# Storing u four times and loading it as 32 rows, partitions ordered images by states

## The chip, the cores and the metric

The kernel runs on one core of a Trainium2 chip. The metric is the device time of one execution in microseconds (us). The program is one launch; all 16 DMA engines of the core and its five instruction queues (PE for matmuls, DVE, ACT, POOL and SP) belong to it alone.

## What is computed

The reference is a network of four layers on an input of 64 images, each of 11 x 11 positions and 128 channels. Every layer has two parts with a residual around each: a mixer, which is the same in all four layers, and a feed-forward part, which differs (a mixture of experts, twice a recurrent net, and a spectral convolution). The change touches the mixer alone. Cut to what matters, it is:

```python
xz = x @ in_proj_w.T                                   # x: 64 images, 121 positions, 128 channels
xc, z = jnp.split(xz, 2, axis=-1)                      # 256 each
xc = conv_general_dilated(xc as (B, 121, 256), conv_w, (1,), [(1, 1)])   # in the kernel: 121 "channels", 256 steps
t = silu(xc + conv_b)
xs = stack([t, t], axis=1)                             # K = 2 directions
x_dbl = einsum('bkdl,kcd->bkcl', xs, x_proj_w)
dts, Bs, Cs = x_dbl[:, :, :8], x_dbl[:, :, 8:24], x_dbl[:, :, 24:]
delta = softplus(einsum('bkrl,kdr->bkdl', dts, dt_proj_w) + dt_proj_b)
A = -exp(A_logs).reshape(2, 121, 16)                   # 16 states
dA = exp(delta[..., None] * A)
dBu = delta[..., None] * Bs * xs[..., None]
h[l] = dA[l] * h[l - 1] + dBu[l]                       # along the 256 steps
y = einsum('bkdln,bknl->bkdl', h, Cs) + Ds * xs
out = layernorm(y[:, 0] + flip(y[:, 1])) * gelu(z) @ out_proj_w.T
```

With `u = delta * t`, the scan's input is `u * B`, where `u` depends on image, channel and step, and `B` on image, state and step. So each row of `u` is needed for all 16 states.

## The kernel before

The mixer is the class `Conv`. It takes the 64 images in 8 groups of `CB` = 8, and each group in two directions, so there are 16 pairs (group `c`, direction `k`), numbered `m`. A scan fills the 128 partitions with 8 images times 16 states. In the order before, partition `p` is state `p // 8` and image `p % 8` (states by images).

For one `m` there are 121 channels, taken in pairs: 61 steps of two channels, 512 elements a partition. A step of the main loop in `run` is:

- `rows` (L677, PE): two matmuls that spread `delta` from the three bf16 parts in `R` onto the 128 partitions of `da`; `pick` holds the matrices that choose the rows.
- `exps` (L690, ACT): two exponentials in place on `da`, with the scale `A`.
- `scan` (L698, DVE): one scan over 512 elements, `da` and `ub` into `H`.
- `by_c` (L719, PE): matmuls of `H` with `Cz`, which sum over states; `keep_y` (L734 DVE, L736 ACT) takes their results out.

`u` reaches the scan by way of DRAM. `steps` computes, for two images at a time, `delta` and `u` with channels on partitions (`u`, L339, on POOL), and its `store` (L353 and L354) writes `delta` to `dD` and `u` to `uD`. `uD` is laid out as `[group, direction, image, 128 channels, 256]`. Then `load_u` (L654) brings 4 channels of all 8 images into one `ub` tile of 128 x 1024 elements: 8 rows of 4096 bytes, repeated for 16 states. There are `UB` = 7 such buffers. `times_b` (L666, POOL) multiplies `ub` in place by `Bt`. For one `m` that makes 31 tiles (30 of 4 channels and one of a single channel).

Other loads of the mixer: `load_bc` (L636) loads `Bt` and `Cp`, both as (state, image) rows from `bcD`; `load_r` (L627, L629) loads `R` from `dD`; `tail` loads `ts` from `sD` (L453) and `y` from `yD` (L455) for the group before, transposes and normalizes them (L460, L468, L474) and projects; `last` (L552 `sD`, L559 `yD`) does that for the last group of a layer. `begin` (L206) loads the next group's `x`.

The order is written out by hand. `at` and `lay` put closures on a plan by step numbers, and `run` plays it: for step `g` the matmuls and exponentials of `g + 3` come first, then `load_u` and `times_b` due at this step, then the scan, then what the plan holds. `load_u` of a tile is put 14 steps ahead of its first scan, `times_b` 5 steps. Each engine executes its own instructions in the order of the program, and all of these DMAs are issued from SP, so a DMA that waits holds those behind it. `steps` of a group's first direction start at step 49 of the group before, 11.6 steps apart for each two images; those of the second direction at 95. In the first group of a layer, `steps(0, 0, ...)` runs ahead of the loop, alone. The tiles `d` and `u` of `steps` have two buffers each.

```python
        self.nc.sync.dma_start(
            x[:, :n, :].rearrange("p d l -> p (d l)"),
            self.uD[m // 2, m % 2, :, 4 * i : 4 * i + n, :]
            .rearrange("b d l -> b (d l)")
            .unsqueeze(0)
            .to_broadcast([NS, CB, n * L]),
        )
```

These are the lines of `load_u` before. The functions that the diff touches follow whole.

Of the kernel before, what the change touches and what calls it, by code (L numbers as in the profile page):

```python
# [8 lines left out]
F32 = mybir.dt.float32  # L9
BF16 = mybir.dt.bfloat16  # L10
AF = mybir.ActivationFunctionType
ALU = mybir.AluOpType
AX = mybir.AxisListType
# [3 lines left out]
D = 121  # L17
C = 128
L = 256
NS = 16  # L20
# [18 lines left out]
def bcast(ap, n):  # L39

    return ap.unsqueeze(2).to_broadcast([ap.shape[0], ap.shape[1], n])
# [36 lines left out]
CB = 8  # L78
# [2 lines left out]
TILES = 31  # L81
STEPS = 2 * PAIRS
RING = 5
UB = 7


class Conv:
# [9 lines left out]
    def weights(self, setup, fixed, ps):  # L97
        cx, nc, a = self.cx, self.nc, self.cx.a
        p = f"L{self.l}_conv_"

        def load(pool, name, shape, src):
            t = pool.tile(shape, F32, name=name)
            nc.sync.dma_start(t, src)
            return t

        in_x = load(setup, "in_x", [128, 2, C], a[p + "in_x"].rearrange("(q p) c -> p q c", p=128))
        conv_wT = load(
            setup, "conv_wT", [128, 3, 2, L], a[p + "conv_wT"].rearrange("j (q p) o -> p j q o", p=128)
        )
        x_dt = load(setup, "x_dt", [8, 2, D], a[p + "x_dt"])  # L110
        dt_wT = load(setup, "dt_wT", [8, 2, D], a[p + "dt_wT"])
        self.Ds = fixed.tile([128, 2], F32, name="Ds")
        nc.vector.memset(self.Ds, 0.0)
        nc.sync.dma_start(self.Ds[:D], a[p + "Ds"])
        self.in_zT = load(fixed, "in_zT", [C, L], a[p + "in_zT"])
        self.conv_b = load(fixed, "conv_b", [1, L], a[p + "conv_b"])
        self.x_bc = load(fixed, "x_bc", [D, 4 * NS], a[p + "x_bc"])
        self.norm = load(fixed, "norm", [D, 2], a[p + "norm"])
        self.out_wT = load(fixed, "out_wT", [128, 2, C], a[p + "out_wT"].rearrange("(q p) c -> p q c", p=128))

        self.A = fixed.tile([128, 2, D], F32, name="A")
        for k in range(2):
            nc.sync.dma_start(self.A[:, k, :], a[p + "A_logs"][k].unsqueeze(1).to_broadcast([NS, CB, D]))
        return lambda: self.made(setup, fixed, ps, in_x, conv_wT, x_dt, dt_wT)

    def made(self, setup, fixed, ps, in_x, conv_wT, x_dt, dt_wT):
        cx, nc, a = self.cx, self.nc, self.cx.a
        p = f"L{self.l}_conv_"
        af = self.A.rearrange("p k d -> p (k d)")
        nc.scalar.activation(af, af, AF.Exp)  # L130
        nc.vector.tensor_scalar_mul(af, af, -1.0)


        pick = setup.tile([5 * 24, 5, CB], F32, name="pick")
        nc.vector.reduce_sum(pick, cx.ident[:120, :120].rearrange("p (a s b) -> p a b s", s=3, b=CB), axis=AX.X)
        self.pick = fixed.tile([5 * 24, 5, NS, CB], BF16, name="pick16")
        for i in range(5):
            nc.vector.tensor_copy(self.pick[:, i], pick[:, i, :].unsqueeze(1).to_broadcast([120, NS, CB]))

        self.w_conv = fixed.tile([C, 3, L], F32, name="w_conv")  # L140
        for j in range(3):
            pw = ps.tile([C, L], F32, name="pw", tag="mm")
            for q in range(2):
                nc.tensor.matmul(pw, in_x[:, q, :], conv_wT[:, j, q, :], start=(q == 0), stop=(q == 1))
            nc.scalar.copy(self.w_conv[:, j, :], pw)


        self.w_dt = fixed.tile([D + 1, 2, 128], F32, name="w_dt")
        nc.vector.memset(self.w_dt, 0.0)
        nc.sync.dma_start(self.w_dt[D : D + 1, :, :D], a[p + "dt_b"].unsqueeze(0))  # L150
        for k in range(2):
            pw = ps.tile([D, D], F32, name="pdt", tag="mm")
            nc.tensor.matmul(pw, x_dt[:, k, :], dt_wT[:, k, :], start=True, stop=True)
            nc.scalar.copy(self.w_dt[:D, k, :D], pw)
        self.one = fixed.tile([128, 1], F32, name="one")
        nc.vector.memset(self.one, 1.0)
        self.ones = fixed.tile([1, 128], F32, name="ones")
        nc.vector.memset(self.ones, 1.0)

        self.own = fixed.tile([128, CB], F32, name="own")  # L160
        nc.vector.reduce_sum(self.own, cx.ident.rearrange("p (n b) -> p b n", b=CB), axis=AX.X)

    def buffers(self, fixed, work, ps_f, dram):
        cx, nc, NC = self.cx, self.nc, self.NC
        self.work = work

        self.H = [fixed.tile([128, 2 * L, 16], F32, name="H"), cx.HX.rearrange("p (a w) -> p a w", w=16)]
        self.spare = [x.rearrange("p a w -> p (a w)") for x in self.H]
        self.da = [ps_f.tile([128, 2, L], F32, name=f"da{i}") for i in range(RING)]
        self.yb = ps_f.tile([128, 8, 2, 2, 16], F32, name="yb")  # L170
        nc.vector.memset(self.yb, 0.0)
        self.Cz = [fixed.tile([128, 64, CB], F32, name=f"Cz{i}") for i in range(4)]
        self.t = fixed.tile([128, CB, L], F32, name="t")
        nc.gpsimd.memset(self.t, 1.0)  # L174
        self.xnT = [fixed.tile([C, CB, D + 2], F32, name=f"xnT{i}") for i in range(2)]
        for x in self.xnT:
            nc.gpsimd.memset(x[:, :, 0 : D + 2 : D + 1], 0.0)
        self.yst = fixed.tile([128, 64, D], F32, name="yst")
        self.uD = dram.tile([NC, 2, CB, 128, L], F32, name="uD")
        self.dD = dram.tile([NC, 2, 128, 3, CB, L], BF16, name="dD")  # L180
        self.bcD = dram.tile([NC, 4 * NS, CB, L], F32, name="bcD")
        self.sD = dram.tile([NC, 128, CB, L], F32, name="sD")
        self.yD = dram.tile([NC, L, CB * D], F32, name="yD")
# [99 lines left out]
    def steps(self, c, k, start, apart, late):  # L283


        nc, work, out = self.nc, self.work, []
        alone = c == 0 and k == 0
        for b in range(0, CB, 2):
            s = {}
# [61 lines left out]

            def store(b=b, s=s):
                nc.sync.dma_start(self.dD[c, k, :, :, b : b + 2, :].rearrange("d s b l -> d s (b l)"), s["d"])  # L353
                nc.sync.dma_start(  # L354
                    self.uD[c, k, b : b + 2].rearrange("b d l -> d b l"), s["u"].rearrange("p (b l) -> p b l", l=L)
                )

            at = start + b // 2 * apart
            for i, f in enumerate((project, parts, e, ln, less, delta, first)):
# [2 lines left out]
            for i, f in ((late, u), (late + 1, rest), (late + 2.5, second), (2 * late + 2, third), (2 * late + 4, store)):  # L362
                out.append((at + i, f))
# [267 lines left out]
    def load_bc(self, m):  # L631
        c, k = m // 2, m % 2
        for name, at in (("Bt", 0), ("Cp", NS)):
            x = self.work.tile([128, L], F32, name=name, bufs=2)
            r0 = 2 * NS * k + at
            self.nc.sync.dma_start(x, self.bcD[c, r0 : r0 + NS].rearrange("r b l -> (r b) l"))  # L636
            self.bc[m, name] = x

    def own_c(self, m, u):
# [9 lines left out]
    def load_u(self, T):  # L649
        m, i = divmod(T, TILES)  # L650
        n = min(4, D - 4 * i)
        x = self.work.tile([128, 4, L], F32, name="ub", bufs=UB)
        self.ub[T] = x
        self.nc.sync.dma_start(  # L654
            x[:, :n, :].rearrange("p d l -> p (d l)"),
            self.uD[m // 2, m % 2, :, 4 * i : 4 * i + n, :]
            .rearrange("b d l -> b (d l)")
            .unsqueeze(0)
            .to_broadcast([NS, CB, n * L]),
        )  # L660

    def times_b(self, T):
# [8 lines left out]
    def rows(self, g):  # L671

        m, p = divmod(g, PAIRS)
        for j in range(self.channels(p)):
            d = 2 * p + j
            n = 24 if d == D - 1 else 120
            self.nc.tensor.matmul(  # L677
                self.da[g % RING][:, j, 1:],
                self.pick[:n, d % 5].rearrange("p n b -> p (n b)"),
                self.R[m, d // 35][:n, d % 35 // 5, 1:],  # L680
                start=True,
                stop=True,
            )

    def exps(self, g):
        m, p = divmod(g, PAIRS)
        for j in range(self.channels(p)):
            x = self.da[g % RING][:, j, 1:]
            d = 2 * p + j
            self.nc.scalar.activation(x, x, AF.Exp, scale=self.A[:, m % 2, d : d + 1])  # L690

    def scan(self, g):
# [6 lines left out]
            self.H[dq % 2][:, :n, p - DQ[dq][0]],  # L699
            self.da[g % RING].rearrange("p j l -> p (j l)")[:, :n],  # L700
            x.rearrange("p d l -> p (d l)")[:, 2 * j * L : 2 * j * L + n],
# [668 lines left out]
def metaformer_kernel(ctx: ExitStack, tc: tile.TileContext, a: dict, out: bass.AP):  # L1370
# [28 lines left out]
    cx.KD = dram.tile([R0[3], C * C], F32, name="KD")  # L1399
    v, kept, passing, weights = mixer(0)  # L1400
    weights()()
    passing.close()
    for l in range(4):
# [70 lines left out]
```

## Time and profile before

| | |
|---|---|
| Median of 3 runs | 8451.34 us (8445.54 to 8459.70) |
| Span of the profiled execution | 8458.2 us, between its first and last instruction |
| Busy PE, DVE, ACT, POOL | 5994.4, 6141.0, 5768.7, 5832.5 us |
| DMA moved | 1603.70 MB, mean 190 GB/s |
| `ub<-uD` loads | 1920 of 512 KB and 64 of 128 KB |
| `uD<-u` stores | 256 of 256 KB |
| `dD<-d` stores, `R<-dD` loads | 256 of 384 KB; 192 of 420 KB and 64 of 180 KB |
| Multiply by B, L666 | 1984, 2317 ns in the mean |
| Scan, L698 | 3904, some 1200 ns each |

The profile shows one execution; its span is 6.9 us over the median of the runs and inside their spread. No other time of that execution is given. Where the profile cuts the span in 40 slices, each is 211 us long. The four mixers with their scans are the stretches from about 80 to 1720, 2090 to 3720, 4038 to 5680 and 5995 to 7620 us; the feed-forward parts and the start of the next mixer lie between and behind.

### The profile page before, as it was taken

How to read it: one execution, taken by the hardware profiler on the slowest of the kernel's cores; microseconds unless marked ns; L12 is line 12 of the kernel's file. 1: busy time of each engine (PE TensorE's matmuls, PEld its weight loads, DVE VectorE, ACT ScalarE, POOL GpSimd, SP SyncE). 2: the span in 40 equal slices, each digit the busy share in tenths (PEclk: the TensorE clock that was granted, in tenths of full speed). 3: DMA queues.
4: the chain of work that ended last, by engine and by line, in shares of the span. 5: the costliest groups of instructions: out<-in, count | busy, mean ns of one | idle time of the engine just before them, and what ended most of it. 6: DMA issues, size and time to landing. Idle time of an engine off the chain costs nothing.

```text
span 8458.2 us, 209204 instructions
## 1 busy us (share of the span) xinstructions
PE 5994.4 (71%) x83374; PEld 3445.8 (41%) x83374; DVE 6141.0 (73%) x8636; ACT 5768.7 (68%) x12927; POOL 5832.5 (69%) x3139
## 2 busy tenths in 40 slices
PE   5676677676677767767677777666567776766999
PEld 3343343355344434344344444344333433433445
DVE  6888888854888888872788888882688888883211
ACT  6888888743888878862788788863688888873210
POOL 6888888921988888850888888870688888890000
PEclk7777777767777777776777777766777778778999
DMA  6888998946898899960899999981689888992111
GB/s 171 221 224 223 223 226 225 232 140 177 218 224 225 224 220 222 230 181 25 222 220 227 221 226 226 224 205 31 179 226 225 230 225 226 226 231 72 39 34 37
DMA packets 933130, 1603.70 MB, mean 190 GB/s; under 512 B 139912, under 2 KB 620514, under 8 KB 932151
## 3 DMA queue, kind: packets, MB, share of 16 engines
q1 hardware_dynamic: 930871, 1588.21, 74.6%
q8 instruction: 655, 10.73, 0.6%
q14 instruction: 324, 2.65, 0.1%
q10 hardware_dynamic: 1280, 2.10, 0.1%
HBM read 1299.53 MB, written 290.52 MB: 188 GB/s over the span
## 4 chain that ended last, share of the span: by engine, by line
PE 31%; ACT 20%; DMA 17%; DVE 14%; issue 8%; POOL 7%; SPq 1%; DVEq 0%; POOLq 0%; ACTq 0%
ACT da L690 7%; DVE H L698 5%; DMA ub<-uD 5%; POOL ub L666 5%; PE da L677 4%; PE yb L719 4%; PE pc L253 4%; DVE HX L698 3%; DMA ts<-sD 3%; PE pu L1306 3%; PE acc L1309 3%; PE out L1349 2%; DMA uD<-u 2%; PE pst L1193 2%; DMA R<-dD 2%
## 5 line engine op out<-in xcount | busy, mean ns | idle before, releaser
L666 POOL TENSOR_TENSOR ub<-ub,Bt 128x1024 f32<-128x1024 f32 (+1 forms) x1984 | 4564.0, 2317 | 731.8 <-DMA ub<-uD 526.1
L690 ACT ACTIVATE da<-da,A 128x255 f32<-128x255 f32 x7744 | 3389.6, 446 | 1094.7 <-PE da L677 918.7
L698 DVE TENSOR_TENSOR_SCAN H<-da,ub 128x512 f32<-128x512 f32 x2048 | 2391.8, 1205 | 93.6 <-POOL ub L666 42.0
L677 PE MATMUL da<-R,pick 120*128 120x255 bf16 x7744 | 1783.5, 324 | 938.0 <-DVE H L698 529.4
L698 DVE TENSOR_TENSOR_SCAN HX<-da,ub 128x512 f32<-128x512 f32 (+1 forms) x1856 | 2115.6, 1187 | 90.5 <-issue 52.4
L677 PEld LDWEIGHTS <-pick 120*128 120x128 bf16 x7744 | 599.6, 104 | 1638.3 <-issue 777.1
L719 PE MATMUL yb<-H,Cz 128*16 128x64 f32 x32768 | 867.6, 255 | 349.8 <-ACT yst L736 260.4
L719 PE MATMUL yb<-HX,Cz 128*16 128x64 f32 x32768 | 856.5, 246 | 209.9 <-ACT yst L736 102.5
L719 PEld LDWEIGHTS yb<-H,Cz 128*16 128x16 f32 x32768 | 604.5, 112 | 921.4 <-issue 520.1
L719 PEld LDWEIGHTS yb<-HX,Cz 128*16 128x16 f32 x32768 | 562.4, 110 | 680.7 <-issue 316.8
L734 DVE TENSOR_TENSOR yst<-yst,yb 128x512 f32<-128x512 f32 (+2 forms) x640 | 340.2, 548 | 272.7 <-PE yb L719 272.5
L253 PE MATMUL pc<-w_conv,xnT 128*121 128x256 f32 x1344 | 441.6, 426 | 55.2 <-ACT t L257 55.1
L174 POOL MEMSET t<- 128x2048 f32 x4 | 7.2, 1804 | 597.4 <-PE px L1200 416.3
L736 ACT COPY yst<-yb 128x512 f32<-128x512 f32 (+2 forms) x640 | 330.6, 543 | 109.3 <-DMA yD<-yst 43.1
L304 PE MATMUL pd<-t,w_dt 122*128 122x512 f32 x480 | 358.3, 839 | 54.6 <-ACT t L264 54.6
L339 POOL TENSOR_TENSOR u<-relu,t 128x512 f32<-128x512 f32 x240 | 307.2, 1280 | 22.7 <-DVE relu L330 22.6
L350 POOL TENSOR_TENSOR d<-relu,d 128x512 bf16<-128x512 f32 x240 | 278.6, 1161 | 54.1 <-ACT d L346 53.9
L1273 DVE COPY U<-pu 128x488 f32<-128x488 f32 x128 | 85.4, 667 | 283.4 <-PE pu L1306 283.4
L1275 ACT COPY U<-pu 128x488 f32<-128x488 f32 x128 | 72.9, 569 | 309.2 <-PE pu L1306 309.2
L343 POOL TENSOR_TENSOR relu<-relu,d 128x512 f32<-128x512 f32 x240 | 279.1, 1163 | 6.6
L253 PEld LDWEIGHTS pc<-w_conv,xnT 128*121 128x121 f32 x1344 | 233.7, 209 | 102.8 <-ACT t L257 81.6
L643 POOL TENSOR_TENSOR Cz<-Cp,own 128x512 f32<-128x512 f32 x256 | 274.4, 1072 | 0.0
(242 smaller groups left out, 7929.8 us busy)
## 6 DMA issues: line engine op xcount, KB each, us to landing
ub<-uD SPq DMA_DIRECT2D x1920, 512.0 KB
dD<-d SPq DMA_DIRECT2D x256, 384.0 KB
R<-dD SPq DMA_DIRECT2D x192, 420.0 KB
uD<-u SPq DMA_DIRECT2D x256, 256.0 KB
sD<-s SPq DMA_DIRECT2D x128, 256.0 KB
yD<-yst SPq DMA_DIRECT2D x512, 60.5 KB
ts<-sD SPq DMA_DIRECT2D x56, 512.0 KB
y<-yD SPq DMA_DIRECT2D x112, 242.0 KB
```

Source lines behind the costliest of these rows:

```text
L253: nc.tensor.matmul(pc, lhs, rhs, start=(j == 0), stop=(j == taps - 1))
L304: nc.tensor.matmul(s["p"], self.w_dt[:, k, :], tb[: D + 1], start=True, stop=True)
L339: nc.gpsimd.tensor_mul(s["u"], s["relu"], tb)
L343: less.tensor_sub(s["relu"], s["relu"], s["d"][:, 0, :])
L350: less.tensor_sub(s["d"][:, 2, :], s["relu"], s["d"][:, 1, :])
L666: self.nc.gpsimd.tensor_mul(x, x, self.bc[m, "Bt"].unsqueeze(1).to_broadcast([128, n, L]))
L677: self.nc.tensor.matmul(self.da[g % RING][:, j, 1:], self.pick[:n, d % 5].rearrange("p n b -> p (n b)"), self.R[m, d // 35][:n, d % 35 // ...
L690: self.nc.scalar.activation(x, x, AF.Exp, scale=self.A[:, m % 2, d : d + 1])
L698: self.nc.vector.tensor_tensor_scan(self.H[dq % 2][:, :n, p - DQ[dq][0]], self.da[g % RING].rearrange("p j l -> p (j l)")[:, :n], x.rearra ...
L719: self.nc.tensor.matmul(self.yb[32 * q : 32 * q + 16, slot % 8, :, :, :w], self.Cz[slot // 8][:, place % 64 : place % 64 + 2, :].rearrange ...
L734: nc.vector.tensor_add(dst, dst, src)
L736: nc.scalar.copy(dst, src)
```

## The change

`uD` gets a dimension more: four copies of `u` for each image. `store` writes `u` four times, with the same tile as source. `load_u` reads all 32 rows (image, copy) and repeats each for four partitions, where before 8 rows were repeated for 16. For that, four neighbouring partitions must need the same image, so the order of partitions becomes images by states: partition `p` is image `p // 16`, state `p % 16`. Everything that knows this order is turned with it: the load of `A`, `pick`, `own`, and the loads of `Bt` and `Cp`. The sizes of the instructions on PE, DVE, ACT and POOL stay, and so does their order; SP issues 768 DMAs more.

```diff
+COPIES = 4
...
-            nc.sync.dma_start(self.A[:, k, :], a[p + "A_logs"][k].unsqueeze(1).to_broadcast([NS, CB, D]))
+            nc.sync.dma_start(self.A[:, k, :], a[p + "A_logs"][k].unsqueeze(0).to_broadcast([CB, NS, D]))
...
-        self.pick = fixed.tile([5 * 24, 5, NS, CB], BF16, name="pick16")
+        self.pick = fixed.tile([5 * 24, 5, CB, NS], BF16, name="pick16")
         for i in range(5):
-            nc.vector.tensor_copy(self.pick[:, i], pick[:, i, :].unsqueeze(1).to_broadcast([120, NS, CB]))
+            nc.vector.tensor_copy(self.pick[:, i], bcast(pick[:, i, :], NS))
...
-        nc.vector.reduce_sum(self.own, cx.ident.rearrange("p (n b) -> p b n", b=CB), axis=AX.X)
+        nc.vector.reduce_sum(self.own, cx.ident.rearrange("p (b n) -> p b n", b=CB), axis=AX.X)
...
-        self.uD = dram.tile([NC, 2, CB, 128, L], F32, name="uD")
+        self.uD = dram.tile([NC, 2, CB, COPIES, 128, L], F32, name="uD")
...
-                nc.sync.dma_start(
-                    self.uD[c, k, b : b + 2].rearrange("b d l -> d b l"), s["u"].rearrange("p (b l) -> p b l", l=L)
-                )
+                for r in range(COPIES):
+                    nc.sync.dma_start(
+                        self.uD[c, k, b : b + 2, r].rearrange("b d l -> d b l"),
+                        s["u"].rearrange("p (b l) -> p b l", l=L),
+                    )
...
-            self.nc.sync.dma_start(x, self.bcD[c, r0 : r0 + NS].rearrange("r b l -> (r b) l"))
+            self.nc.sync.dma_start(x, self.bcD[c, r0 : r0 + NS].rearrange("r b l -> b r l"))
...
-            self.uD[m // 2, m % 2, :, 4 * i : 4 * i + n, :]
-            .rearrange("b d l -> b (d l)")
-            .unsqueeze(0)
-            .to_broadcast([NS, CB, n * L]),
+            self.uD[m // 2, m % 2, :, :, 4 * i : 4 * i + n, :]
+            .rearrange("b r d l -> (b r) (d l)")
+            .unsqueeze(1)
+            .to_broadcast([CB * COPIES, NS // COPIES, n * L]),
...
-                self.pick[:n, d % 5].rearrange("p n b -> p (n b)"),
+                self.pick[:n, d % 5].rearrange("p b n -> p (b n)"),
```

## Prediction

> **What bounds the kernel now.** I read the busy shares by slice first, then the waits, then the four scan stages alone, then the traffic of single transfers.
>
> ```profile
> DMA  6888998946898899960899999981689888992111
> GB/s 171 221 224 223 223 226 225 232 140 177 218 224 225 224 220 222 230 181 25 222 220 227 221 226 226 224 205 31 179 226 225 230 225 226 226 231 72 39 34 37
> ```
> ```profile
> 80.00:1720.00 1640.00, 1142.60 (x19291) 641.23 (x19290) 1397.67 (x1762) 1308.51 (x2922) 1438.64 (x767) 0.77 0.88 223
> 2090.00:3720.00 1630.00, 1139.68 (x19219) 640.30 (x19219) 1394.21 (x1758) 1306.37 (x2917) 1438.61 (x767) 0.77 0.91 224
> 4038.00:5680.00 1642.00, 1152.06 (x19356) 647.13 (x19355) 1402.51 (x1766) 1313.15 (x2928) 1439.16 (x768) 0.76 0.92 223
> 5995.00:7620.00 1625.00, 1132.14 (x19356) 638.66 (x19355) 1397.43 (x1763) 1309.08 (x2925) 1438.18 (x767) 0.78 0.89 225
> ```
>
> The second fence is the table of stretches, one scan stage a line: length, then busy us of PE, PE loads, DVE, ACT and POOL, the clock, the DMA share and GB/s. The four stages hold 6537 of 8458 us, and in each the DMA engines are busy 0.88 to 0.92, POOL 1438, DVE 1397 and ACT 1309 of some 1635. No engine is full; several are close, and they are coupled by order. Which of them sets the pace is seen in the waits:
>
> ```profile
> POOL ub L666 <- DMA ub<-uD: 526.1, 402, 13.4
> PEld L677 <- DMA R<-dD: 122.6, 35, 21.1
> PE pk L460 <- DMA ts<-sD: 112.7, 33, 6.1
> DVE y L468 <- DMA y<-yD: 90.5, 23, 8.2
> ```
> ```profile
> SPq L654 <- DVE H L698: 1974.9, 913, 8.9
> SPq L654 <- DMA uD<-u: 98.5, 30, 5.1
> ```
> ```profile
>   DVE H L698: 42.0, 11
>   DVE HX L698: 10.8, 9
> ```
>
> POOL often waits for a `ub` load, but the last fence (who waited for POOL's multiply L666) shows that the scans lost only 42.0 + 10.8 us to it. SP waits 1974.9 us for scans to free a `ub` buffer: POOL runs ahead, and its waits are mostly slack. From the trace, I get a median of 7.9 us between a tile's multiply and its first scan, 2.9 us at the fifth percentile. So DMA is nearly full, but the pace is set by the coupled order of DVE, ACT and PE; DMA reaches it through loads that PE and DVE take directly.
>
> **What a `ub` load gets.** Three stretches in the same columns:
>
> ```profile
> 71.25:71.75 0.50, 0.00 (x0) 0.00 (x0) 0.00 (x0) 0.00 (x0) 0.00 (x0) 0.50 1.04 305
> 2084.00:2096.00 12.00, 4.84 (x20) 2.61 (x20) 6.58 (x7) 9.67 (x22) 8.95 (x4) 0.50 1.04 240
> 3729.00:3729.50 0.50, 0.50 (x25) 0.50 (x29) 0.00 (x0) 0.50 (x1) 0.00 (x0) 0.50 1.11 446
> ```
>
> From 2084 to 2096 only `ub` loads move: all 16 engines are full, at 240 GB/s, and the rate is the same before the multiplies start, so compute on SBUF is not the cause. At 3729 the end of the stage loads `sD` (L552): packets of 4096 bytes into 128 partitions as for `ub`, but from 128 different rows, at 446. The packet records say 159 ns as median for those and 245 for `ub`. What differs is the source: 16 engines read the same 8 rows.
>
> **What the Trainium skill says.** "DMA: Bandwidth & Descriptors", Queues, rings and completion order: the DMAs of one issuing engine go through one ring on each DMA engine, in order. The trace agrees: one queue moves 1588 of 1604 MB, and a load behind a store lands late. The same page, Why a DMA increments its semaphore by 16 and not by 1: a DMA runs on the largest k up to 16 that divides both slowest sizes. So `ub` keeps 16 (32 rows to 128 partitions), and the reordered Bt and Cp loads fall from 16 to 8 (8 images); no run here shows that. Its Latency and other measured facts has copies of 16 KiB rows slow down at pitches of 2 MiB and more, not at 512 KiB. The new pitch is 128 KiB, but with 4 KiB rows; here `HX<-mid`, 4 KiB rows at a pitch of 32 KiB, ran at means of 186 to 243 ns a packet at the end of the first three layers, so distinct rows alone do not ensure 159. The page has no line for one row read by many engines.
>
> **The change part by part.**
>
> 1. `ub` loads. 1920 x 512 KB + 64 x 128 KB = 1015 MB. At 240 GB/s they take 4.23 ms of all engines' time. At the 330 that I take (between 240 and 446: the first packets of each load, and other traffic, stay slow) it is 3.08 ms: 1.15 ms less. At 240 nothing is saved; below that, it costs.
> 2. Stores. Three more `uD<-u` for each of 256: 768 x 256 KB = 201 MB. Stores move at about 340 GB/s (packets of 1024 bytes at 46 ns), so 0.77 us each and 0.59 ms in all. Parts 1 and 2 balance at 1015 / (4.23 - 0.59) = 279 GB/s. At 330 DMA has 0.56 ms less to do of 5.88 (the four shares times their lengths), a share of 0.81.
> 3. What that is worth. Loads taken directly by PE and DVE: `ts` 33 waits, `y` 23, `R` 31 (without the four at stage starts), `x` 27. Each stands behind about two `ub` loads, 0.6 us shorter each, and its own packets speed up too; so I cut 1.7 us from those of `ts` and `y`, 1 from the others: 56 + 39 + 31 + 27 = 153. Half I let reach the end (-76), because DVE's next item is often as late by PE or ACT. Of the 526 us at POOL half goes; on scans that is 26, and as much through PE's wait for POOL: -51.
> 4. Stage starts. There `steps` runs alone, with two `u` buffers. The timeline of the second layer:
>
> ```profile
> 2067.40 1.28 POOL L339 TENSOR_TENSOR u<-H,t 128x512 f32<-128x512 f32 x1 [6.01 <-DMA uD<-u]
> 2073.02 1.29 POOL L339 TENSOR_TENSOR u<-H,t 128x512 f32<-128x512 f32 x1 [4.34 <-DMA uD<-u]
> ```
>
>    The third and fourth `u` wait for the stores of the first and second. Those land 3 x 0.77 = 2.3 us later, and the last four stores stand ahead of R and the first `ub`. The two delays partly overlap: 4 us a layer, +16.
> 5. Bursts. Each of 240 later stores holds SP by 3 x 0.6 us (median issue 615 ns) and the rings by 2.3 us more. Queued behind are the next `ub` loads, which have POOL's 7.9 us of lead, and in perhaps one of four of the 114 waits above a direct load: 29 x 2.3 x half = +33. SP gives its DMAs eight completion semaphores in turn, so an issue waits for the eighth before it; five in place of two shorten that window, from some 15 us of issues to 11, still over the loads' usual 6 to 9 us.
> 6. The first `ub` of an image group waits for the last `uD` store (98.5 us, 30 waits): 30 x 2.3 us later at SP, covered by POOL's lead except for a quarter: +17.
> 7. The new order of A, `pick`, `own` and of the 128 Bt and Cp loads: no other instruction of PE, ACT, DVE or POOL is added. The Bt and Cp loads may take 0.6 us longer each, 18 steps ahead of use: 0, hidden by that distance.
>
> Sum: -76 - 51 + 16 + 33 + 17 = -61 on a profiled span of 8458.2. The median of the runs is 8451.3, 7 us below the span, so I forecast 8390.
>
> **The rivals.**
>
> A, the source of slowness is not the shared row but the pitch: rows at 128 KiB compete for the same part of memory, and `ub` stays at 240. `HX<-mid` speaks for it; against it, 121 rows there go by 11 engines by the rule above, and one of the three layers kept 186 ns. DMA then has 5.88 + 0.59 = 6.47 ms to do in 6.54. The busiest stages show 0.92, and I allow 0.95: 6.81 ms, +270, with starts +16: about 8740. It decides from `ub` below 279 GB/s. With `ub` slower than before, over 8800.
>
> B, DMA is relieved but was no bound: direct waits only move to ACT and PE, and the burst terms remain: -25 + 66, with some given back, 8470 to 8490. For it: scans lose only 53 us to POOL.
>
> C, DMA is the true bound behind the coupling, and all its direct waits in the stages (about 300) and the scans' 53 go: 8451 - 353 + 66 = about 8165, if nothing else is late; half of that, 8300, is as far as I go. Against it: ACT and PE wait for each other for longer than for DMA.
>
> That nothing changes in the load's rate because the row is still read by many engines is excluded by the order: 32 rows, four partitions each, 16 engines.
>
> **How the numbers follow.** Forecast (parts 1 to 7) 0.42, C 0.08, B 0.18, A 0.32. The forecast case has its own range of 8310 to 8450: `ub` at 300 to 400 GB/s, and a quarter to all of the shortened waits counted. A measurement of this kernel tells 0.2%, 17 us, from no change. Faster: most of the first case and C, 0.47; same: its edge and that of B, 0.12; slower: A and most of B, 0.41. The range goes from C's 8290 to 8790, which takes in A at 240 GB/s, and leaves out about 2 in 10.
>
> **What would show it.** Right: stretches of `ub` alone at over 300 GB/s, the stages' DMA share near 0.8, fewer waits for `ts`, `y` and `ub`, and stage starts some 4 us longer. Wrong: `ub` alone still near 240 and shares over 0.95 (A); or 400 and the same stage lengths (B). If the waits for `uD<-u` at SP or POOL grow by over 100 us, part 5 was too small.

## The result, and the profile after

The changed kernel takes 8477.39 us (median of 6 runs, 8461.42 to 8492.03), the kernel before 8438.13 us (6 runs, 8429.46 to 8459.70; three of them are those of the table ahead). The ratio is 1.0043 with a 95% interval of 1.0028 to 1.0058: slower by some 36 to 39 us, where I had forecast faster by 61. Beside the later kernels the kernel before has medians of 8445 to 8461 us, so the size of the difference is less sure than this interval says; its sign stands against each of them. The profiled execution of before was the slowest of its six runs and that of after the fastest of its own, so the two spans (8458.2 and 8459.6 us) are nearly equal. These two traces show where time is spent, but the size of the difference comes from the runs alone.

The slices of the page and the four scan stages (columns as before: length, busy us of PE, PE loads, DVE, ACT and POOL, clock, DMA share, GB/s):

```profile
DMA  6888888856788888851788888870688888882111
GB/s 198 248 254 256 257 255 254 265 151 190 247 253 256 256 257 252 260 177 45 242 252 256 256 257 254 258 225 31 206 255 251 258 253 256 253 260 72 41 32 37
```
```profile
80.00:1720.00 1640.00, 1141.88 (x19356) 642.11 (x19355) 1402.29 (x1766) 1317.44 (x2935) 1440.61 (x768) 0.77 0.82 252
2090.00:3720.00 1630.00, 1154.03 (x19486) 647.30 (x19488) 1395.28 (x1763) 1309.97 (x2915) 1429.87 (x764) 0.76 0.81 252
4038.00:5680.00 1642.00, 1160.02 (x19614) 652.06 (x19614) 1399.09 (x1769) 1311.18 (x2917) 1431.39 (x765) 0.76 0.81 251
5995.00:7620.00 1625.00, 1152.26 (x19277) 647.52 (x19277) 1388.22 (x1752) 1302.87 (x2906) 1429.49 (x764) 0.76 0.81 252
```

The DMA engines are busy 0.81 to 0.82 of the stages in place of 0.88 to 0.92, and move 252 GB/s in place of 224: more bytes in less time. A stretch at the start of the second layer, where only `ub` loads move, shows why (same columns):

```profile
2077.00:2087.00 10.00, 4.07 (x16) 2.24 (x17) 5.25 (x6) 8.03 (x19) 7.63 (x4) 0.50 1.01 388
```

388 GB/s, where the same loads had 240. Over all `ub` packets of 4096 bytes in the records, one takes 159 ns in the median and 209 in the mean; in the kernel before, counted the same way, 248 and 265. So the change does what it says. The waits of the kernel after (who waited for what: us in total, times, longest):

```profile
POOL ub L669 <- DMA ub<-uD: 546.5, 345, 15.2
PEld L680 <- DMA R<-dD: 139.5, 26, 25.6
ACT yst L739 <- DMA yD<-yst: 94.3, 26, 6.5
POOL u L340 <- DMA uD<-u: 49.6, 8, 8.8
PE pk L463 <- DMA ts<-sD: 44.8, 21, 6.4
DVE y L471 <- DMA y<-yD: 8.4, 4, 2.5
```
```profile
SPq L657 <- DVE H L701: 1614.4, 810, 8.7
...
SPq L657 <- DMA uD<-u: 83.5, 68, 3.8
```

The direct waits for `y` and `ts` shrank: DVE's for `y` from 90.5 to 8.4 us, PE's for `ts` from 112.7 to 44.8. POOL's for `ub` did not, from 526.1 to 546.5. Others grew: R from 122.6 to 139.5, and ACT's wait for the stores `yD<-yst`, which the prediction doesn't mention, to 94.3. In the kernel before it was:

```profile
ACT yst L736 <- DMA yD<-yst: 43.1, 18, 4.1
```

By my own sign for it (waits for `uD<-u` at SP or POOL over 100 us longer), part 5 was large enough: SP's went from 98.5 to 83.5, POOL's from 41.9 to 49.6. The sign looked in the wrong place, as the experiments show.

### The profile page after: what moved, and what is told of

It is laid out like the page before. It is cut to its first block, busy times and chain, and to the rows that moved or that the text cites. A ratio compares the mean times of both kernels' runs of the same rounds, so it can differ in the third digit from the quotient of the medians.

```text
span 8459.6 us, 210104 instructions
## 1 busy us (share of the span) xinstructions
PE 6024.2 (71%) x83374; PEld 3451.4 (41%) x83374; DVE 6136.2 (73%) x8636; ACT 5778.1 (68%) x12927; POOL 5829.9 (69%) x3139
## 4 chain that ended last, share of the span: by engine, by line
PE 32%; ACT 20%; DVE 14%; DMA 14%; issue 8%; POOL 8%; SPq 4%; DVEq 0%; POOLq 0%; ACTq 0%
ACT da L693 7%; DVE H L701 5%; POOL ub L669 5%; PE da L680 5%; PE yb L722 4%; PE pc L254 4%; DVE HX L701 3%; DMA ub<-uD 3%; PE acc L1312 3%; PE pu L1309 3%; PE out L1352 3%; DMA ts<-sD 2%; DMA R<-dD 2%; PE pst L1196 2%; PE po L517 2%
## 5 line engine op out<-in xcount | busy, mean ns | idle before, releaser
L669 POOL TENSOR_TENSOR ub<-ub,Bt 128x1024 f32<-128x1024 f32 (+1 forms) x1984 | 4561.5, 2321 | 683.3 <-DMA ub<-uD 546.5
L701 DVE TENSOR_TENSOR_SCAN H<-da,ub 128x512 f32<-128x512 f32 x2048 | 2395.4, 1209 | 114.6 <-POOL ub L669 48.8
L701 DVE TENSOR_TENSOR_SCAN HX<-da,ub 128x512 f32<-128x512 f32 (+1 forms) x1856 | 2117.4, 1190 | 113.9 <-issue 80.4
L739 ACT COPY yst<-yb 128x512 f32<-128x512 f32 (+2 forms) x640 | 330.8, 543 | 131.8 <-DMA yD<-yst 94.3
```

The costliest lines, as they stand in the source:

```text
L669: self.nc.gpsimd.tensor_mul(x, x, self.bc[m, "Bt"].unsqueeze(1).to_broadcast([128, n, L]))
L701: self.nc.vector.tensor_tensor_scan(self.H[dq % 2][:, :n, p - DQ[dq][0]], self.da[g % RING].rearrange("p j l -> p (j l)")[:, :n], x.rearra ...
L739: nc.scalar.copy(dst, src)
```

## The experiments

Two theories stood at first: that the relief of the loads is worth about what I forecast and the three stores more cost far more than I priced; or that the relief is worth little and the stores about what I priced (rival B). Where an expectation numbers theories, this is their order. Rival A had fallen already with the 388 GB/s. Each kernel has a short name (e1 to e12), by which the expectations refer to it. All ratios below are to runs of the kernel before that stand beside it, with their 95% interval; "by the ratio" means the difference in ratio times the time before. The lines of the later kernels are shifted by a few: the scan is L701 or L705, ACT's copy into `yst` L739 or L743.

### Loads alone, stores alone

Loads alone, first version (e1); `u` is stored once:

```diff
-        self.uD = dram.tile([NC, 2, CB, COPIES, 128, L], F32, name="uD")
+        self.uD = dram.tile([NC, 2, CB, 128, L], F32, name="uD")
...
-            self.uD[m // 2, m % 2, :, :, 4 * i : 4 * i + n, :]
-            .rearrange("b r d l -> (b r) (d l)")
+            self.uD[m // 2, m % 2]
+            .rearrange("b (r e) l -> (b r) e l", r=COPIES)[:, 4 * (i % 7) : 4 * (i % 7) + n, :]
+            .rearrange("b e l -> b (e l)")
```

> The new loads without the new stores: u is stored once as before, and each ub load reads 32 rows, of other channels of the same image (4 x (i mod 7), 32 channels apart), so it reads the wrong u; order of partitions as after. T1 (the prediction's: direct waits for DMA reach the end, only the stores' cost was too small): DMA share falls to 0.72 and the time to 8438 - 127 = about 8310. T2 (rival B: DMA was no bound): DMA share 0.72 all the same, waits for ts and y fall by over half, and the time stays within 20 us of before, 8415 to 8440.

Measured: 8342.89 us against 8461.20, ratio 0.9868 [0.9853, 0.9884]: 112 us faster by the ratio. DMA share 0.73 to 0.75. `ub` packets 159 ns in the median, 216 in the mean.

Stores alone (e2), on the kernel before; `load_u` reads copy 0 of each image as it did:

```diff
+                for r in range(COPIES):
+                    nc.sync.dma_start(
+                        self.uD[c, k, b : b + 2, r].rearrange("b d l -> d b l"),
...
-            self.uD[m // 2, m % 2, :, 4 * i : 4 * i + n, :]
+            self.uD[m // 2, m % 2, :, 0, 4 * i : 4 * i + n, :]
```

> The new stores without the new loads: u is stored four times, ub is loaded from the first copy in the old way, old order of partitions. DMA share about 0.98. T1: as the direct waits reach the end, they grow with the fuller rings: 8650 or more. T2: the stores cost what they cost after (stage starts +15, bursts +25) plus somewhat more as the rings are fuller: 8480 to 8560.

Measured: 8623.03 us, ratio 1.0199 [1.0183, 1.0214]: 168 us slower. That lies between the two theories, below 8650 and above 8480 to 8560. Two of the stages:

```profile
80.00:1720.00 1640.00, 1143.39 (x18779) 637.16 (x18778) 1368.74 (x1731) 1292.57 (x2881) 1413.61 (x756) 0.75 0.97 249
2090.00:3720.00 1630.00, 1111.18 (x18135) 618.35 (x18135) 1336.38 (x1704) 1268.07 (x2811) 1372.04 (x736) 0.75 0.95 248
```

Loads alone at the changed kernel's own distance between rows (e8): only group 0 stores four copies, and all groups read them.

```diff
-                for r in range(COPIES):
+                for r in range(COPIES if c == 0 else 1):
...
-            self.uD[m // 2, m % 2, :, :, 4 * i : 4 * i + n, :]
+            self.uD[0, m % 2, :, :, 4 * i : 4 * i + n, :]
```

> The loads of after with its rows 128 KiB apart, and one store for each block but in the first group of a layer, where the four copies are stored; later groups load the first group's u, which is the wrong u. So an eighth of the additional stores is left. If the rows' distance does not matter: as e1 with an eighth of the 148 us, about 0.989 of before. If 32 KiB was what slowed e1's packets (mean 209 ns against 185): 0.975 to 0.985, and the stores cost after some 170 to 240 us.

Measured: 8336.84 us against 8452.98, ratio 0.9866 [0.9853, 0.9878]: 113 us faster; `ub` packets 159 ns in the median, 215 in the mean. The means in the expectation (209 and 185) do not come out when all packets are counted: they are 216 for the first loads-alone kernel and 209 for the changed one, so no difference between the packets has to be explained. The first two stages, and the waits:

```profile
80.00:1720.00 1640.00, 1140.12 (x19698) 647.60 (x19696) 1416.59 (x1830) 1326.72 (x2963) 1444.77 (x772) 0.78 0.77 230
2090.00:3720.00 1630.00, 1135.77 (x19489) 649.99 (x19489) 1400.60 (x1906) 1306.16 (x2930) 1398.26 (x747) 0.78 0.74 225
```
```profile
POOL ub L669 <- DMA ub<-uD: 399.3, 269, 15.0
PE pk L463 <- DMA ts<-sD: 67.5, 28, 4.5
DVE H L701 <- POOL ub L669: 62.3, 12, 15.2
DVE y L471 <- DMA y<-yD: 15.5, 5, 3.6
```

What follows: the relief is real and reaches the end. Rival B's mechanism is refuted, although its time (8470 to 8490) holds the measured one. The distance between the rows costs nothing that shows (0.9868 and 0.9866). From 0.9866 to 1.0043 it is 1.77%, by the ratio 150 us (some 16 either way; 141 by the medians), which the stores of groups 1 to 7 take back. I had priced them at 33 + 17 = 50. One thing more differs: in this kernel the loads of the later groups wait for no store of their own group (SP's wait for `uD<-u` at `load_u` is 2.6 us, after 83.5). What that is worth is tested below.

### What of the stores costs

Two copies instead of four (e3):

```diff
-COPIES = 4
+COPIES = 2
```

> COPIES = 2: 16 rows to eight partitions each, one store more in place of three. ub loads at 160 to 200 ns a packet if each engine reads a row of its own; a third of the stores' cost. T1: 8340 to 8380. T2: 8438 + 38/3 = about 8450, same as before within 0.2%.

Measured: 8496.98 us, ratio 1.0045 [1.0032, 1.0057], slower than either theory had it. DMA share 0.89 to 0.90, `ub` packets 239 ns in the median and 254 in the mean: with two copies the loads are hardly faster, so there is little relief to set against the one store more. It doesn't tell how the price grows with the number of stores, since the relief changed with it.

The same bytes in half the issues (e4), one DMA an image, with four repeats:

```diff
-                for r in range(COPIES):
+                for i in range(2):
...
-                        self.uD[c, k, b : b + 2, r].rearrange("b d l -> d b l"),
-                        s["u"].rearrange("p (b l) -> p b l", l=L),
+                        self.uD[c, k, b + i].rearrange("r d l -> d r l"),
+                        s["u"][:, i * L : i * L + L].unsqueeze(1).to_broadcast([128, COPIES, L]),
```

> As after, but each block of u is stored by two DMAs (one an image, its four copies by a repeated source) and not by four: the same bytes and packets, half the issues on SP. If the cost of bursts is SP's time and its semaphore window: about half of the 38 us back, 8455 to 8465. If it is the bytes in the rings: 8477 as after.

Measured: 8488.63 us, ratio 1.0038 [1.0024, 1.0052], the changed kernel's own within the interval. Not the number of issues at SP, then.

Copies that nobody reads (e6), so that no load can wait for them; the loads are those of the first loads-alone kernel:

```diff
+        self.uX = dram.tile([NC, 2, CB, COPIES - 1, 128, L], F32, name="uX")
...
+                for r in range(COPIES - 1):
+                    nc.sync.dma_start(
+                        self.uX[c, k, b : b + 2, r].rearrange("b d l -> d b l"),
```

> The loads of e1 (32 rows of other channels, wrong u) with the three more stores of after, into a tensor that nobody reads; so no load waits for them, and the loads' rows lie as in e1. If the stores alone make the difference between e1 and after: 8470 to 8490. If it is the wait of the loads for the later copies, or the rows' greater distance (128 KiB in place of 32): near e1, 8340 to 8380.

Measured: 8545.38 us, ratio 1.0102 [1.0088, 1.0117]. The price is there though SP's wait for `uD<-u` at `load_u` is only 29.9 us, so it isn't that wait (part 6). Why it is even higher than in the changed kernel stays open; the packets do not tell (214 ns in the mean against 209). ACT's wait for `yD<-yst` is 114.4 us here, once more high.

The copies 1 to 3 issued by ACT instead of SP (e7):

```diff
...
+                for i in range(2):
+                    nc.scalar.dma_start(
+                        self.uD[c, k, b + i, 1:].rearrange("r d l -> d r l"),
+                        s["u"][:, i * L : i * L + L].unsqueeze(1).to_broadcast([128, COPIES - 1, L]),
```

> As after, but the three more copies are issued by ACT (two DMAs for each block of u), so they pass through other rings than the loads of SP. ACT pays 512 x 0.45 = 230 us for issues. If loads are late because they stand behind the stores in SP's rings, that cover is gone and the waits for ub, ts and yD fall back to e1's; the time is 8380 to 8480, as ACT's share allows. If the bytes count: 8500 or more.

Measured: 8615.94 us, ratio 1.0195 [1.0181, 1.0209].

```profile
ACT yst L743 <- DMA yD<-yst: 139.1, 23, 8.2
```

This run mixes several things: ACT issues 512 DMAs (418 ns each in the median), and SP now waits 495.4 us at `load_u` for the copies of `u`, in place of 83.5, and 68.3 us for them at the `yD` stores. So ACT's queue, used in this way, is no way out, but the run doesn't tell whether the order on SP's queue is what costs. Other queues were not tried.

### Where the stores stand

The four stores of a block stand together, right behind that of `d`. Each kernel from here on moves them on the plan only: number, bytes and loads stay. In the code, `store` keeps the DMA of `d`, and the copies become closures of their own, laid at steps of the plan:

```diff
+            for r in range(COPIES):
+                i = late + 2 + (late + 2) * r / (COPIES - 1)
+                out.append((at + i, lambda f=copy, r=r: f(r)))
```

This is the version at even steps (e5) from two steps behind `u` on, the last copy at the store of `d`:

> As after, the same bytes, but the four stores of u are not issued together behind that of d: they are laid at four even steps from two steps after u is made to the step of d's store, so none comes later than after. T3 (the stores cost by coming as a block of 3.3 us in the rings, behind which loads are late): most of the 148 us between loads alone and after come back, 8350 to 8400. T4 (the stores cost by their bytes, wherever they stand): 8460 to 8490.

Measured: 8411.79 us against 8445.12, ratio 0.9949 [0.9937, 0.9962].

All four together, but at one earlier step (e9; the lines are compared with those of e5):

```diff
-                i = late + 2 + (late + 2) * r / (COPIES - 1)
+                i = late + 2 + (late + 2) / 3
```

> As e5, but the four stores of u stand together again, at one step some four after u is made (for the later groups), apart from d's store. If the length of a block in the rings counts (four stores 3.1 us, with d's 4.2): 0.998 to 1.003 of before. If it was only that the copies stood at the latest step, just ahead of loads that wait for them: as e5, 0.995.

Measured: 8403.48 us, ratio 0.9945 [0.9932, 0.9959]. Both are faster than the changed kernel, and alike within the interval. That spread or together is the same doesn't follow from it: the table below has their losses at different places.

Spread, and all of them ahead of the store of `d` (e10; again compared with e5):

```diff
-                i = late + 2 + (late + 2) * r / (COPIES - 1)
+                i = late + 2 + late * r / (COPIES - 1)
```

> As e5, but the last of the four stores comes one to two steps ahead of d's store and not in the same step. If a shorter block and an earlier landing give more: 0.990 to 0.994 of before; if the bytes set the rest: 0.995 as e5.

Measured: 8391.35 us, ratio 0.9931 [0.9918, 0.9945].

So the same stores cost 150 us in one place and about 55 to 70 in others. To see what they hit, I took from each trace the time from a scan's start to the next, summed over blocks of six steps of a group, as a mean over the groups 1 to 6 and the four layers. The table gives the difference to loads alone (the second version), in us a group:

```
steps                  24-29  30-35  90-95  114-119   all 122
before                  1.03   2.04   0.63    0.85      4.93
after                   1.73   0.67   0.42    1.40      5.02
half the issues         1.89   0.73   0.68    1.33      5.45
even steps              0.47   0.71   0.09    1.41      3.32
early, together        -0.10   0.35  -0.04    2.62      3.29
spread, all ahead       1.05   0.79  -0.04    0.38      3.12
one block moved (e11)   0.62   0.21   0.86    1.53      3.87
last version (e12)      0.05   0.11  -0.07   -0.07      0.67
```

The last two rows are kernels of the next part. In most blocks that are not listed the scans of all these kernels run at the same pace, most within 0.1 us, the largest difference 0.5. The time is lost at two places. At steps 24 to 35 the kernel before pays for the late `y` and `ts` of `tail` (DVE's and PE's waits for them stand there, 3.1 and 3.4 us a group); the change takes most of that away (30 to 35) and pays at 24 to 29 instead. The other place is the end of a group.

### Which waits they are

Steps 24 to 35 in the timeline of after (start, us, engine, line, what; in brackets the idle time before and its releaser), group 2 of the second layer:

```profile
2541.11 3.49 SPq L356 DMA_DIRECT2D uD<-u  x4
2543.11 0.67 ACT L739 COPY yst<-yb 128x512 f32<-128x512 f32 x1
2544.64 3.21 SPq L754 DMA_DIRECT2D yD<-yst  x4
2551.22 0.65 ACT L739 COPY yst<-yb 128x512 f32<-128x512 f32 x1 [3.63 <-DMA yD<-yst]
2552.01 0.80 PE L722 MATMUL yb<-H,Cz 128*16 128x64 f32 x24 [2.58 <-ACT yst L739]
2552.76 1.23 DVE L701 TENSOR_TENSOR_SCAN HX<-da,ub 128x512 f32<-128x512 f32 x1 [3.30 <-issue]
```

`yst` (L179) is one tile for a whole group. The group before still has to go from it to `yD` (L754) when ACT begins to write the next one into it (L739). The third block of `u` stores of the second direction is laid 18.2 steps into the group and goes out right ahead of the last `yD` stores. They land later, ACT waits 3.63 us, PE's matmuls 2.58, and the scan, which by the order of the code needs a free `HX`, 3.30 (the profile names no releaser for it, which is what `issue` means).

To test this, only that one block of eight is moved, to step 12.9 (e11):

```diff
+                i = late + 2 + (late + 2) / 3 if k == 1 and b == 4 and late == 6 else 2 * late + 4
```

> The changed kernel, but of the eight blocks of four u stores of a group only one is moved: the third of the second direction goes from 18.2 steps into the next group to 12.9, so that it no longer stands right ahead of the last yD stores. Number of stores, their order among themselves and the loads stay. Theory of the named wait (late stores hold up the yD stores, ACT waits for them before it may write yst, PE and the scan wait for ACT): the step blocks 24 to 35, which cost the changed kernel 2.4 us a group over the loads alone, fall to 0.3 to 0.7; ACT's wait for yD falls from 94 to about 45 us; 24 groups with 1.7 to 2.1 us: about 40 to 50 us, ratio to before 0.998 to 1.000. Rival (the cost comes from the amount of stores, wherever they stand): the wait moves elsewhere, ratio stays 1.003 to 1.006.

Measured: 8447.85 us against 8446.91, ratio 0.9999 [0.9990, 1.0008]; the changed kernel had 1.0043, so by the ratio 37 us less (some 15 either way; 30 by the medians). The blocks 24 to 29 and 30 to 35 fall from 1.73 and 0.67 to 0.62 and 0.21: 1.57 us in 24 groups, 38 us. The waits of this kernel:

```profile
ACT yst L743 <- DMA ub<-uD: 40.3, 16, 6.8
ACT yst L743 <- DMA yD<-yst: 32.8, 13, 6.5
```
```profile
DVE HX L705 <- issue: 44.1, 20, 5.1
```

In after the two waits of ACT were 5.1 and 94.3, and that of the scans:

```profile
DVE HX L701 <- issue: 80.4, 28, 5.2
```

ACT's sum falls by 26 us only, since part of it is now put down to `ub` loads, but the scans' wait falls by 36.3 us. So the loss at this place is as large as the gain in the runs. The two traces as wholes don't show that gain: steps 90 to 95 rise by 0.44 us a group, so that all 122 steps fall by 1.15 (28 us in 24 groups), and the spans are alike (8459.6 and 8460.4 us), that of after being its fastest run and this one the slowest of 13. A second buffer for `yst`, which would test the same wait from its other end, was not tried.

The end of a group in the early version (four stores together):

```profile
2666.79 2.89 SPq L357 DMA_DIRECT2D uD<-u  x4
2669.78 0.97 SPq L634 DMA_DIRECT2D R<-dD  x1
2676.37 0.11 PEld L684 LDWEIGHTS <-pick 120*128 120x128 bf16 x2 [3.01 <-DMA R<-dD]
2676.38 0.39 PE L684 MATMUL da<-R,pick 120*128 120x255 bf16 x2 [2.84 <-DMA R<-dD]
```

Here the first block of the second direction goes out ahead of the load of R for the next group, and PE waits 3 us for R. In the whole trace:

```profile
PEld L684 <- DMA R<-dD: 166.2, 32, 23.3
```

The last kernel (e12) is this version with that block alone 1.6 steps later, behind R:

```diff
-                i = late + 2 + (late + 2) / 3
+                i = late + 2 + (late + 2) / 3 + (1.6 if k == 1 and b == 0 and late == 6 else 0)
```

> The version with all blocks early (four stores together, ahead of the store of d), but the first block of the second direction 1.6 steps later, behind the load of R for the next group instead of ahead of it. Theory of the named wait (in the early version PE waits for R behind that block, 2.6 us of 3.3 us a group over the loads alone): the step block 114 to 119 falls from +2.6 to under +0.8 and the total from 3.3 to about 1.3 us a group; 24 to 28 groups with 2 us: 48 to 56 us less than the early version's 0.9945, ratio to before 0.988 to 0.990. Rival (stores cost where they are put, whatever waits there): ratio stays 0.993 to 0.996.

Measured: 8330.68 us against 8446.91, ratio 0.9870 [0.9855, 0.9885]. That is 63 us less than the early version; in the table, steps 114 to 119 fall from +2.62 to -0.07, which in 24 groups is 65 us, and the whole from 3.29 to 0.67. Its waits for R, and its first two stages:

```profile
PEld L684 <- DMA R<-dD: 98.5, 10, 23.6
```
```profile
80.00:1720.00 1640.00, 1149.98 (x19665) 651.51 (x19665) 1416.18 (x1817) 1324.73 (x2957) 1441.35 (x772) 0.77 0.84 255
2090.00:3720.00 1630.00, 1132.17 (x19546) 647.54 (x19539) 1400.52 (x1899) 1304.73 (x2928) 1402.41 (x749) 0.79 0.82 252
```

The 10 waits for R that are left are mostly at the starts of the layers, with up to 23.6 us each. All 1024 stores are there, the DMA share is near that of after, and the time is that of loads alone (0.9866), now with the right `u`: well placed, the three stores more cost nothing that the runs can tell (3 us by the ratio, some 16 either way; the table leaves 0.67 us a group, 16 us in 24 groups). This version beats the kernel before by 1.3%.

## Why the prediction was wrong

- **Part 1, the loads**: right. I took 330 GB/s; `ub` alone has 388 over 10 us, and 240 times the ratio of the mean packets (265 to 209 ns) is 304. The share of 0.81 came out as worked out. One reading ahead of it was wrong: the half microsecond before the multiplies start has 305 GB/s, not the same rate as the 240 behind it, so that line did not exclude the work on SBUF as a cause. The 388 with POOL busy for 7.63 of the 10 us does.
- **Part 2**: right. A store's packets take 46 ns in the median, as before.
- **Part 3 and POOL, -127**: right in sum, but not in its terms, so the close hit is partly luck. Loads alone are 113 us faster with the longer stage starts in them, and 127 with these added back; the first version, which has no longer starts, gives 112. Of the direct waits, DVE's for `y` all but went and PE's for `ts` fell to 67.5 us in loads alone, and steps 24 to 35, where they stand, give 3.07 us a group, 74 us in 24 groups. R did not gain in the kernel after. The 51 us by way of POOL are not seen: its wait for `ub` fell to 399.3 us in loads alone, not to half, and the scans that the prediction has waiting 42.0 + 10.8 us for POOL wait 62.3 + 1.8 there.
- **Part 4, stage starts, +16**: right. From the first `uD<-u` to the first scan it is 29.0 us in the mean of the four layers, 25.5 before: 3.5 a layer, 14 in all.
- **Parts 5 and 6, +33 and +17**: here the prediction failed. The runs show some 150 in place of 50, and that turned a gain into a loss. I counted the blocks as a random hit on loads: one in four of 114 waits, at half of 2.3 us. But the plan repeats itself in every group, so a block that stands ahead of a critical transfer does so 24 times or more. And I counted only loads: the direct wait that grew most is for a store, `yD<-yst` (43.1 to 94.3 us), which ACT waits for because `yst` is one buffer. The prediction asked what is queued behind the new DMAs on SP, but not who waits for a *store* that is queued there. The Trainium skill, "DMA: Bandwidth & Descriptors", Queues, rings and completion order, says what was needed, that each DMA engine takes up what one issuer has put on its ring in order; I used it for loads alone. The trace fits: the `yD` stores that went out right behind four `u` stores kept ACT waiting for 3.63 us. Of the 150 us the runs name 37 (`yD`, by moving one block). The end of the group has 1.67 us a group in steps 108 to 119, 40 us in 24 groups, with waits for R just behind it; that part was tested in the early version and not in the changed kernel itself. That placing the stores removes the price, as far as the runs can tell, is shown; a share for each of the other places isn't, and about half of the 150 stays without a name.
- **Part 7, the new order**: nothing seen against it. `Bt` and `Cp` take 1.0 and 1.1 us from first to last packet in the median, in place of the 1.4 and 2.0 of before. They didn't get longer but shorter.
- **The rivals**: A fell with the 388 GB/s and with loads alone at the same pitch. B has the right time by two wrong terms: it lost the relief that is there, and underpriced the stores. C's 8300 wasn't reached by any kernel, but the best one (8331) is nearer to it than to the forecast.

## What to carry to other kernels

A DMA that is added to a repeating plan must be priced at its place: list what follows it on its queue, stores too, and for each who needs it landed (also for a buffer to come free), and how soon. If the mechanism gains and the sum doesn't, run its halves apart before doubting it, as loads alone and stores alone do here. A trace cut into the steps of the loop, and compared with the half that gained, shows the few places where the new work is in the way, and moving it there may cost nothing.

## What the hardware showed that I had not expected

- Two copies don't bring half the relief: read from 8 rows, a packet of `ub` takes 248 ns in the median, from 16 rows 239, from 32 rows 159. Most of it comes with the last doubling.
- The granted clock differs a little by kernel: 0.769 to 0.772 in the runs of after, 0.773 to 0.783 in before, 0.781 to 0.785 in the best version, 0.783 to 0.791 in loads alone. Whether it is a cause of the times or follows from them was not tried.
